# Splitting a second block product once more, and moving masking and att + beta I to another engine, in a four-layer graph network kernel

## The chip, the cores and the metric

The kernel runs on one core of a Trainium2 chip. A core has five engines with a queue each: PE (TensorE, matrix products), DVE (VectorE), ACT (ScalarE), POOL (GpSimd) and SP (SyncE, which here issues all DMAs). Each engine works its own queue strictly in order and waits on semaphores for the others. The metric is the device time of one execution in microseconds; shown is the median of several runs.

## The reference, cut to what matters

```python
def reference(x, adj, W0, bias0, b1, Wq, Wk, Wv, W3, a, beta):   # x: (128, 128, 512), adj: (128, 128), float32
    # layer 0: deg = adj.sum(1); nadj = adj * deg^-1/2 (rows and columns)
    x = layernorm(x + nadj @ (x @ W0) + bias0)
    # layer 1: A = adj @ x, C = adj @ x + b1; out[o, i] = max over j of relu(A[o, j] + (C - A)[o, i])
    x = layernorm(x + out)
    # layer 2: rel = adj.T * (q @ k.T), each row divided by its norm
    x = layernorm(x + rel(x) @ (x @ Wv.T))
    # layer 3: h = x @ W3; e = leaky_relu(s1 + s2.T) * adj; att = softmax(e)
    x = layernorm(x + elu(att @ h + beta * h))
    return x
```

x is 128 matrices of 128 x 512 (nodes by features). Since both weights of layer 1 are the same, C - A is the bias alone, out is the same along each row, and the normalization takes it out again; the kernel folds layer 1 into the variance of the normalization before it (1 + EPS in `var`). In layer 2, q k^T = x (Wq^T Wk) x^T, so one product with a matrix G = Wq^T Wk serves for both. In layer 3, att h + beta h = (att + beta I) h.

## The kernel before, in words

**Groups and steps.** The 128 matrices go in 32 groups of four (GB = 4). `Group` holds the steps of one group, each a method with a short name: y (nadj x), w (times W0), z (times G), r (rel = z x^T), v (times Wv^T), f (rel times v), k (times W3) and h ((att + beta I) times k) are TensorE's; the others are the work around them. "3.ej" in a schedule is step ej of the group that is 3 after the base.

**The order is written out.** HEAD, TURN and TAIL are strings of such steps. The loop at the end (`for base, steps in ...`) runs HEAD, then TURN for each group from FIRST to NG + LAST - 1, then TAIL; each instruction is put on its engine's queue in that order, and nothing reorders it. FIRST is 10 and LAST -5, so TURN runs 17 times, and HEAD and TAIL hold similar stretches written out.

**Block products.** w, z, v and k are products of a 512 x 512 activation (four matrices side by side, two by two blocks of 256 x 256) with a 512 x 512 weight. `Product` computes each by Winograd's form with seven block products in place of eight. The sums of blocks that it takes are on the left side `Left.sum` (GpSimd, tiles S, four of 128 x 512), on the weight side `w_sum` (once, VectorE). `Product.make(i)` does block product i: four matrix products of 128 x 256, each in two instructions. Products 6, 3 and 4 are accumulated onto the banks of 1, 5 and 7 (ONTO). The results are put together from PSUM by c (ScalarE copy), d (VectorE addition), t (ScalarE copy of bank 1 with 6 in it) and u (GpSimd addition).

**The second level.** Block product 2 is split once more by the same form in all of w, z, v and k: `make_small` does four 128 x 128 products (step z2), then ScalarE copies half of the bank to q (`before`, bz2), VectorE makes three operations in the bank (`between`, ez2: two of 128 x 128, one of 128 x 384), and three more 128 x 128 products are accumulated onto it (step z28). The left side's four small sums are `Left.small` (GpSimd, lx2, ly2, ln2; tile L, two buffers); the weight's are `w_small_sums` (VectorE, once).

**Attention of layer 3.** sc multiplies x by two vectors, sums (VectorE, the product itself goes to the scratch tile prod) and leaves s. pw writes s to DRAM and pe reads it back, spread over all partitions (both on SP). pl is the leaky relu (ScalarE), ej the masking with adj (VectorE, L428 by the helper tt), ei the row maximum, ex the exponential, rd the reciprocal of the sum, so0 to so3 att * rden + beta I, one matrix each (VectorE, L1067). at, aw, cat bring the result transposed back through DRAM. In layer 2, sq squares rel for its norm into a scratch tile sq.

**Memory.** PSUM has six rotating banks for products. The sbuf pool `mid` holds e, prod, q, t, rel and the like, one buffer each; aT (the transposed activation) and S have three. Between layers the activation is transposed by VectorE in 32 x 32 squares and put in place by 16 DMAs (xd and nd; `Squares.move`).

**Helpers.** Operations of helpers carry the helper's line: L425 copy (ScalarE), L428 tt (VectorE), L431 pool_tt (GpSimd), L434 inv_sqrt (GpSimd, step pow and others).

Of the kernel before, what the change touches and what calls it, by code (L numbers as in the profile page):

```python
# [46 lines left out]
GB = 4  # L47
# [3 lines left out]
FIRST = 10  # L51
LAST = -5
# [3 lines left out]
0.cy11 1.y10 0.cy01 0.sy0 1.y00 1.cy10 0.ly2 1.y11 1.cy00 1.y01 1.cy11 s.s00 0.w1 1.cy01 0.sy2  # L56
0.w5 s.s01 s.s02 s.s03 0.w7 0.dw1 0.sy3 0.dw5 s.sa0 0.dw7 s.m02 s.sk0 0.w2 s.sa1 0.w6 0.bw2
0.ew2 s.sa2 0.w3 0.tw s.sk2 s.sk1 0.w28 0.dw3 s.sa3 0.w4 0.dw2 0.bi01 s.g1 0.dw4 0.bi00 s.sk3
s.g2 s.cg1 s.vt0 0.bi10 s.vt1 s.g5 0.bi11 3.ld s.dg2 2.ld s.vt2 0.uw01 s.vt3 s.g7 s.cg5 s.vd
s.q00 0.stw0 0.uw10 s.g6 s.dg7 0.uw11 0.stw1 s.g3 s.q01 s.tg 0.stw2 1.sy0 s.g4 0.stw3 1.sy1  # L60
s.dg3 1.w1 0.vaw 1.ly2 s.dg4 1.w5 1.dw1 0.pow s.q02 1.w7 0.nbw 1.dw5 1.sy2 0.apw0 0.apw1 1.w2
1.dw7 s.ug11 0.apw2 1.w6 0.xt0 0.apw3 1.sy3 0.xt1 1.bw2 1.tw 0.xt2 1.bi10 1.w3 0.xt3 1.bi00
1.ew2 0.xd s.sg0 1.w28 s.sv0 1.w4 s.sg1 s.sg2 2.y10 s.sg3 2.y00 2.cy10 s.sv1 s.mg2 2.y11 2.cy00
2.cy11 s.sv2 s.sv3 1.dw3 1.bi11 1.dw2 2.y01 1.bi01 1.dw4 2.cy01 3.y10 s.mv2 3.y00 3.cy10 s.q03
3.y11 3.cy00 s.q10 3.y01 3.cy11 s.q11 0.z1 3.cy01 s.q12 s.q13 s.s30 s.wd 0.cz1 s.bi 0.sx0 s.s31
0.z5 s.s32 s.s33 0.cz5 0.sx1 s.wb s.m32 0.z7 0.lx2 0.dz7 0.sx2 0.z2 s.wc0 1.uw01 0.z6 0.bz2
s.wc1 0.ez2 0.sx3 4.ld 1.stw0 1.uw10 0.z3 1.stw1 1.uw11 0.z28 0.z4 2.sy0 0.dz2 0.tz 1.stw2
0.uz11 0.dz3 0.dz4 0.r0 2.sy1 1.stw3 0.r1 2.ly2 1.vaw 0.r2 0.r3 1.pow 0.v1 0.rm 2.sy2 0.rt 0.sq0
0.sq1 0.wr 0.v5 0.cv1 1.nbw 2.sy3 1.apw0 1.apw1 1.xt0 2.bi10 0.v7 0.cv5 1.xt1 1.apw2 0.cr 2.bi00
0.v2 0.dv7 1.apw3 1.xt2 2.bi11 0.v6 0.bv2 0.sq2 0.ev2 0.sq3 2.bi01 0.v3 1.xt3 0.tv 3.sy0 0.v28  # L70
0.dv3 0.uv11 0.v4 0.dv2 3.sy1 0.f0 1.xd 0.dv4 3.ly2 0.f1 0.f2 3.sy2 0.f3 2.w1 0.rp 3.sy3 0.fa0
2.w5 2.dw1 3.bi10 0.fa1 0.fa2 2.w7 3.bi00 2.dw5 0.fa3 3.bi11 2.w2 2.dw7 2.w6 3.bi01 2.bw2 0.stv0
2.ew2 2.w3 2.tw 0.stv1 2.uw01 0.stv2 2.w28 1.sx0 0.stv3 2.w4 2.dw3 1.sx1 2.dw2 1.z1 2.dw4 1.lx2
2.stw0 1.z5 2.stw1 1.cz1 1.sx2 0.vav 1.z7 2.uw10 1.cz5 1.sx3 1.z2 1.dz7 2.uw11 1.z6 1.bz2 1.ez2
0.pov 1.z3 2.stw2 1.tz 1.uz11 2.stw3 1.z28 2.vaw 1.dz3 2.pow 1.z4 1.dz2 2.nbw 0.nbv 2.apw0 1.r0
1.dz4 2.apw1 2.xt0 1.r1 2.apw2 2.xt1 1.r2 2.apw3 2.xt2 0.apv0 1.r3 2.xt3 0.apv1 1.v1 0.sc00 2.xd
0.apv2 1.rm 0.apv3 0.sc01 1.v5 1.cv1 1.rt 1.sq0 0.sc10 1.sq1 1.v7 0.sc11 1.cv5 1.sq2 0.sc20
1.sq3 1.v2 0.sc21 1.rp 1.dv7 1.v6 1.bv2 1.ev2 1.v3 0.sc30 1.tv 1.uv11 0.sc31 1.v28 1.dv3 1.wr
1.v4 1.dv2 0.pw 3.w1 1.dv4 0.nt0 2.sx0 1.cr 3.w5 0.nt1 2.sx1 3.dw1 0.nt2 3.w7 2.sx2 0.pe 3.dw5
# [205 lines left out]
def kernel(  # L285
# [910 lines left out]
```

## Time and profile before

| | us |
|---|---|
| median of three runs | 2032.43 (2029.44 to 2034.14) |
| the profiled execution | 2034.25 |
| its span | 2032.4 |
| TensorE waiting for others, first 100 us | 13.7 |
| TensorE waiting, 1950 to 2000 | 4.5 |
| queue of SP, time its DMAs take as share of 16 DMA engines | 41.7% |

Where the page names a line, it is one of the listing; "out<-in" are the program's tile names with numbers left out (S_x are the block sums of x, L_x the small sums, p_z a PSUM bank of product z, pl_k one of h, C_z the finished z). The number after x counts instructions. A matmul row's "us" goes from its first instruction's start to the modelled end of its last, and overlaps the next row by some 0.15 us, so that the distance of two starts is its price when TensorE is full. "[2.08 <-PE p_z L567]" is idle time before a row, and what ended it.

### The profile page before, as it was taken

What the parts mean: (1) busy time and instruction counts of PE and PEld (TensorE: products, weight loads), DVE (VectorE), ACT (ScalarE), POOL (GpSimd) and SP (SyncE); (2) the same over time, 40 slices, a digit from 0 to 9 for tenths busy, and PEclk for the clock granted to TensorE, in tenths of its full rate; (3) what the DMA queues carried; (4) which work ended last, traced back from release to release, by engine and by line L of the source; (5) the groups of instructions that cost most, each with busy time, mean ns of one, the idle gap of its engine ahead of it and who ended that gap; (6) DMA issues with size and microseconds to landing.
All of it is one profiled execution on the core that took longest, in us unless ns stands there. A gap on an engine that the chain in (4) does not pass through costs nothing.

```text
span 2032.4 us, 31901 instructions
## 1 busy us (share of the span) xinstructions
PE 2004.9 (99%) x10573; PEld 1713.8 (84%) x10573; DVE 1642.7 (81%) x3464; ACT 807.9 (40%) x1739; POOL 1175.9 (58%) x1223
## 2 busy tenths in 40 slices
PE   9899999999999999999999999999999999999997
PEld 8788888888888888888888888888888888888885
DVE  6777888888887888788888878788778888888787
ACT  2223444443343443343433443433434434343344
POOL 7665664656555666556565556565555664676341
PEclk9999999999999999999999999999999999999999
DMA  7234433543345433434433435333444334344423
GB/s 224 63 56 81 94 89 78 110 91 80 69 99 119 105 89 69 88 92 107 95 87 64 100 93 109 91 74 76 97 101 104 87 63 97 87 102 76 77 64 88
DMA packets 737970, 184.71 MB, mean 91 GB/s; under 512 B 689936, under 2 KB 690320, under 8 KB 737808
## 3 DMA queue, kind: packets, MB, share of 16 engines
q1 hardware_dynamic: 737664, 182.56, 41.7%
q8 instruction: 85, 1.39, 0.3%
q14 instruction: 77, 0.63, 0.1%
q10 hardware_dynamic: 144, 0.13, 0.0%
HBM read 64.55 MB, written 49.87 MB: 56 GB/s over the span
## 4 chain that ended last, share of the span: by engine, by line
PE 93%; DVE 2%; DMA 2%; SPq 1%; ACT 1%; issue 0%; POOL 0%; DVEq 0%; ACTq 0%; POOLq 0%
PE p_z L603 16%; PE p_v L603 15%; PE p_w L603 15%; PE p_k L603 15%; PE pr L942 5%; PE pl_v L991 5%; PE py L773 5%; PE pl_k L991 5%; PE p_z L567 2%; PE p_k L567 2%; PE p_v L567 2%; PE p_w L567 2%; SPq L512 1%; DMA s<-d_s 1%; PE pk L864 1%; DMA d_wa<-wa 0%
## 5 line engine op out<-in xcount | busy, mean ns | idle before, releaser
L833 ACT ACTIVATE x<-x,nb,r 128x512 f32<-128x512 f32 x383 | 284.4, 805 | 77.1 <-DVE nb L827 76.9
L431 POOL TENSOR_TENSOR x<-x,bias_bc 128x512 f32<-128x512 f32 x128 | 161.7, 1275 | 99.7 <-PE py L773 85.2
L431 POOL TENSOR_TENSOR C_k<-C_k,t_k 128x512 f32<-128x512 f32 x31 | 40.0, 1290 | 247.1 <-ACT t_k L425 210.0
L434 POOL TENSOR_TENSOR r<-v,minus_half 128x4 f32<-128x4 f32 (+1 forms) x99 | 99.6, 1006 | 133.9 <-DVE v L819 83.8
L1010 DVE SCALAR_TENSOR_TENSOR prod<-x,wa_bc 128x512 f32<-128x512 f32 x256 | 172.6, 674 | 4.5 <-ACT x L833 0.7
L428 DVE TENSOR_TENSOR x<-p_w,x 128x512 f32<-128x512 f32 x192 | 129.2, 684 | 41.0 <-PE p_w L603 37.0
L431 POOL TENSOR_TENSOR x<-x,t_w 128x512 f32<-128x512 f32 x96 | 120.8, 1284 | 34.7 <-ACT t_w L425 31.1
L425 ACT COPY C_z<-p_z 128x512 f32<-128x512 f32 x64 | 37.4, 584 | 249.2 <-PE p_z L603 249.1
L958 ACT ACTIVATE sq<-rel 128x128 f32<-128x128 f32 x128 | 39.7, 310 | 214.2 <-DVE rel L428 212.3
L773 PEld LDWEIGHTS py<-nadjT,x 128*128 128x128 f32 x1024 | 120.6, 194 | 3.4 <-DVE nadjT L671 0.8
L603 PE MATMUL p_z<-S_x,gq_t 128*128 128x256 f32 x512 | 121.2, 379 | 1.2 <-POOL S_x L431 1.2
L603 PE MATMUL p_w<-w_t,S_y 128*128 128x256 f32 x512 | 122.2, 382 | 0.0
L773 PE MATMUL py<-nadjT,x 128*128 128x128 f32 x1024 | 121.2, 277 | 0.5 <-DVE nadjT L671 0.4
L603 PE MATMUL p_z<-S_x,gq 128*128 128x256 f32 x512 | 121.1, 379 | 0.6 <-POOL S_x L431 0.6
L603 PE MATMUL p_k<-w,S_n 128*128 128x256 f32 x496 | 118.9, 383 | 2.7 <-DVE x L1104 2.7
L603 PE MATMUL p_v<-wvT_t,S_x 128*128 128x256 f32 x512 | 121.0, 379 | 0.0
L603 PE MATMUL p_v<-wvT,S_x 128*128 128x256 f32 x512 | 121.0, 379 | 0.0
L603 PE MATMUL p_w<-w,S_y 128*128 128x256 f32 x512 | 121.0, 379 | 0.0
L603 PE MATMUL p_k<-w_t,S_n 128*128 128x256 f32 x496 | 117.2, 379 | 0.0
L991 PE MATMUL pl_k<-C_k,attT 128*128 128x512 f32 x248 | 111.6, 592 | 0.0
L991 PE MATMUL pl_v<-C_v,relT 128*128 128x512 f32 x248 | 111.5, 592 | 0.0
L603 PEld LDWEIGHTS p_z<-S_x,gq 128*128 128x128 f32 x512 | 97.2, 190 | 14.2 <-POOL S_x L431 1.0
(1857 smaller groups left out, 5281.9 us busy)
## 6 DMA issues: line engine op xcount, KB each, us to landing
out_dram<-x SPq DMA_DIRECT2D x127, 256.0 KB, 2.6
x<-in_x_dram SPq DMA_DIRECT2D x31, 1024.0 KB, 5.3
d_r<-ru SPq DMA_DIRECT2D x31, 256.0 KB, 2.0
relT<-d_r SPq DMA_DIRECT2D x124, 64.0 KB, 2.5
s<-d_s SPq DMA_DIRECT2D x31, 256.0 KB, 5.4
d_a<-au SPq DMA_DIRECT2D x31, 256.0 KB, 2.0
attT<-d_a SPq DMA_DIRECT2D x124, 64.0 KB, 2.5
x<-in_x_dram SPq DMA_DIRECT2D x2, 512.0 KB, 4.5
```

Source lines behind the costliest of these rows:

```text
L425: nc.scalar.copy(o, i)
L428: nc.vector.tensor_tensor(o, a, b, f)
L431: nc.gpsimd.tensor_tensor(o, a, b, f)
L434: nc.gpsimd.tensor_tensor(o, v, minus_half[:, : v.shape[-1]], ALU.pow)
L567: nc.tensor.matmul(self.banks[i][:, r, bass.ts(c, P)], lhsT=lhsT, rhs=rhs, start=(not then and n == 0), stop=(n == len(steps) - 1), skip_g ...
L603: nc.tensor.matmul(ps[:, j, :], lhsT=lhsT, rhs=rhs, start=(i not in ONTO and j == 0 and kc == 0), stop=(j == 1 and kc == 1), skip_group_ch ...
L773: nc.tensor.matmul(o, lhsT=self.x_chunk(b, kc), rhs=nadjT, start=True, stop=True)
L833: nc.scalar.activation(xt, xt, AF.Identity, bias=self.nb[k][:, b : b + 1], scale=self.rstd[k][:, b : b + 1],)
L942: nc.tensor.matmul(self.pr[:, b, :], lhsT=self.whole["z"][:, fc, b // 2, bass.ts(b % 2, P)], rhs=self.xT.chunk(b, fc), start=(fc == 0), st ...
L958: nc.scalar.activation(scratch, self.rel[:, b, :], AF.Square, accum_out=self.n2[:, b : b + 1])
L991: nc.tensor.matmul(ps, lhsT=left[:, b, :], rhs=self.whole[k][:, b, :], start=True, stop=True)
L1010: nc.vector.scalar_tensor_tensor(prod, self.x[:, b, :], 1.0, wide(wa_bc[k]), ALU.mult, ALU.mult, accum_out=self.s[:, k, b : b + 1],)
```

## The change

Six things change:

1. Block product 1 of z and of v (layer 2) is split once more, in the way product 2 is: steps lx1 (GpSimd), z1 as four small products, bz1, ez1, z18; v1, bv1, ev1, v18. Small sums of the weights for it (mg1, mv1) are made once. The L tile is now one buffer of eight small blocks for x.
2. For y and n the small sums no longer have a tile: they lie in block (1, 0) of the transposed activation, which nothing reads after the first-level sums (`Left.room`).
3. Masking (ej) is GpSimd's, and att * rden + beta I is two GpSimd operations over all four matrices (so0, so1) in place of four VectorE operations; in the last group it stays with VectorE.
4. Group 0 has no second level in any product.
5. Scratch tiles go: sc's products go to e, Square's output goes into the PSUM bank pr that rel was read from. Some small tiles have two buffers in place of four.
6. The order is written anew: FIRST = 5, LAST = -6 (TURN runs 21 times). In a turn, TensorE's order was z, y, h, r, w, v, k, f (of groups 4, 5, 2, 4, 5, 4, 3, 4) and is z, r, w, v, y, h, k, f (of groups 4, 4, 5, 4, 6, 2, 3, 4). Product 2 stands third among the block products of z and v, not fourth.

```diff
-FIRST = 10
-LAST = -5
+FIRST = 5
+LAST = -6
...
 TURN = """
-4.z1 4.lx2 3.fa3 3.stv1 4.z5 4.cz1 4.sx2 3.stv2 3.stv3 4.sx3 4.z7 4.cz5 3.vav 3.pov 4.z2 4.dz7
-3.nbv 4.z6 4.bz2 3.apv0 4.ez2 3.apv1 4.z3 3.nt0 4.tz 3.sc00 3.apv2 4.uz11 3.nt1 3.apv3 4.z28
...
+4.z1 1.fin2 3.fa3 4.sx1 1.fin3 4.z5 4.bz1 3.stv0 4.sx2 4.ez1 4.z2 2.so0 3.stv1 4.z18 4.bz2 6.ld
+4.ez2 4.z7 4.cz1 4.sx3 4.cz5 3.stv2 2.so1 4.z6 4.dz7 3.stv3 4.z28 4.tz 2.at 4.z3 4.uz11 4.dz2
+2.aw 3.vav 3.pov 4.z4 4.dz3 3.nbv 3.apv0 2.cat 4.r0 4.dz4 3.apv1 3.nt0 4.r1 3.apv2 3.sc00 3.apv3
+4.r2 3.nt1 4.r3 3.nt2 5.w1 3.nt3 4.rm 3.nd 3.sc01 4.sq0 5.w5 4.sq1 5.dw1 4.sq2 4.rt 4.sq3 5.w7
+4.rp 5.dw5 3.sc10 3.sc11 5.w2 5.dw7 5.w6 5.bw2 3.sc20 5.ew2 5.w3 5.tw 3.sc21 5.uw01 3.sc30 5.w28
+5.uw10 5.dw3 5.w4 5.dw2 4.wr 5.uw11 3.sc31 4.v1 5.dw4 3.pw 4.v5 5.stw0 4.bv1 3.sn0 4.ev1 4.cr
+4.v2 5.stw1 3.sn1 4.v18 4.bv2 5.stw2 4.v7 4.cv1 3.sn2 3.pe 4.ev2 4.cv5 3.ln2 4.v6 5.stw3 4.dv7
+3.sn3 5.vaw 4.v28 4.tv 4.v3 3.pl0 4.dv2 5.pow 3.pl1 3.pl2 3.pl3 4.uv11 4.v4 5.nbw 4.dv3 3.ej
+5.apw0 6.y10 4.dv4 5.apw1 5.xt0 6.y00 6.bi10 5.apw2 3.ei 6.y11 5.apw3 5.xt1 6.bi00 6.y01 6.cy00
+5.xt2 6.cy10 6.bi11 2.h0 5.xt3 6.cy11 5.xd 2.h1 6.cy01 2.em0 6.sy0 3.ex0 2.h2 2.em1 2.ee0 6.sy1
...
-    def w_small(w, m):
-        b = lambda k, j: w[:, 2 + k, bass.ts(j, P)]
+    def w_small(w, m, i):
+        b = lambda k, j: w[:, 2 * (i - 1) + k, bass.ts(j, P)]
...
-    w_m = {k: wts.tile([P, 3, P], F32, name=f"m_{k}") for k in "0gv3"}
-    W2 = {k: w_small(weights[k][0], m) for k, m in w_m.items()}
+    SMALL = ("02", "g1", "g2", "v1", "v2", "32")
+    w_m = {k: wts.tile([P, 3, P], F32, name=f"m_{k}") for k in SMALL}
+    W2 = {k: w_small(weights[k[0]][0], m, int(k[1])) for k, m in w_m.items()}
...
         def small(self, i):
-            a = lambda b, k: self.chunk(b, 2 + k)
-            self.l = big.tile([P, 4, P], F32, tag="L", name=f"L_{self.name}", bufs=2)
-            s = [self.l[:, n] for n in range(4)]
+            a = lambda b, k: self.chunk(b, 2 * (i - 1) + k)
+            s = self.room(i)
...
-            self.smalls = dict(
+            self.smalls[i] = dict(
...
+        def room(self, i):
+            return [self.chunk(2 + n // 2, n % 2) for n in range(4)]
...
+    class Shared(Squares):
+        def room(self, i):
+            if i == 1:
+                self.l = big.tile([P, 2, 4, P], F32, tag="L", name=f"L_{self.name}", bufs=1)
+            return [self.l[:, i - 1, n] for n in range(4)]
...
         def make(self, i, then=None):
-            if i == 2 and self.weight in W2:
+            if i in self.left.smalls:
                 self.make_small(i, then is not None)
...
-            self.xT, self.nT = Squares(f"x_{g}"), Squares(f"n_{g}")
+            self.xT, self.nT = Shared(f"x_{g}"), Squares(f"n_{g}")
...
-            scratch = mid.tile([P, P], F32, tag="sq", name=f"sq_{self.g}_{b}")
             nc.scalar.activation(
-                scratch, self.rel[:, b, :], AF.Square, accum_out=self.n2[:, b : b + 1]
+                self.pr[:, b, :], self.rel[:, b, :], AF.Square, accum_out=self.n2[:, b : b + 1]
             )
...
-            prod = mid.tile([P, D], F32, tag="prod", name=f"prod_{self.g}_{b}_{k}")
+                self.e = mid.tile([P, GB, P], F32, tag="e", name=f"e_{self.g}")
             nc.vector.scalar_tensor_tensor(
-                prod,
+                wide(self.e),
...
         def ej(self):
-            tt(self.e, self.e, adj_b, ALU.mult)
+            pool_tt(self.e, self.e, adj_b, ALU.mult)
...
-        def so(self, b):
-            nc.vector.scalar_tensor_tensor(
-                self.e[:, b, :], self.e[:, b, :], self.rden[:, b : b + 1], beta_i, ALU.mult, ALU.add
-            )
+        def so(self, i):
+            if self.end:
+                e, rden = self.e[:, i, :], self.rden[:, i : i + 1]
+                nc.vector.scalar_tensor_tensor(e, e, rden, beta_i, ALU.mult, ALU.add)
+            elif i == 0:
+                pool_tt(self.e, self.e, self.rden.unsqueeze(2).to_broadcast([P, GB, P]), ALU.mult)
+            else:
+                pool_tt(self.e, self.e, beta_i.unsqueeze(1).to_broadcast([P, GB, P]))
```

In HEAD, the w of group 0 is 1 5 7 2 6 3 4 without 28, y of group 3 moves from before z of group 0 to after its f, and d_wa/a_bc (wd, wb) and the copies wc0, wc1 stand in this order:

```diff
-3.y11 3.cy00 s.q10 3.y01 3.cy11 s.q11 0.z1 3.cy01 s.q12 s.q13 s.s30 s.wd 0.cz1 s.bi 0.sx0 s.s31
-0.z5 s.s32 s.s33 0.cz5 0.sx1 s.wb s.m32 0.z7 0.lx2 0.dz7 0.sx2 0.z2 s.wc0 1.uw01 0.z6 0.bz2
-s.wc1 0.ez2 0.sx3 4.ld 1.stw0 1.uw10 0.z3 1.stw1 1.uw11 0.z28 0.z4 2.sy0 0.dz2 0.tz 1.stw2
...
+1.dw2 2.y01 1.bi01 1.dw4 2.cy01 s.sv3 s.q11 s.q12 s.q13 s.s30 s.wd s.bi 1.uw01 0.z1 s.s32 1.stw0
+0.sx0 0.cz1 1.stw1 0.sx1 0.z5 s.wb s.mg1 0.z2 0.cz5 s.s31 0.sx2 0.z7 0.dz2 s.mg2 s.wc0 0.z6
+0.dz7 0.sx3 s.wc1 4.ld s.s33 0.z3 1.uw10 0.z4 1.uw11 2.sy0 0.tz 1.stw2 0.dz3 0.uz11 0.dz4 0.r0
```

## The prediction

> **What bounds the kernel now.** I read first the busy times, then the engines over the middle of the run, then TensorE's timeline through one turn.
>
> ```profile
> PE 2004.9 (99%) x10573; PEld 1713.8 (84%) x10573; DVE 1642.7 (81%) x3464; ACT 807.9 (40%) x1739; POOL 1175.9 (58%) x1223
> ```
> ```profile
> 600.00:1834.00 1234.00, 1233.22 (x6580) 1057.50 (x6579) 1009.23 (x2118) 503.46 (x1083) 744.72 (x775) 1.00 0.43 91
> ```
> ```profile
> 1023.32 1.89 PE L603 MATMUL p_z<-S_x,gq_t 128*128 128x256 f32 x8
> 1025.05 1.89 PE L603 MATMUL p_z<-S_x,gq 128*128 128x256 f32 x8
> 1026.78 0.38 PE L567 MATMUL p_z<-x_16T,gq 128*128 128x128 f32 x2
> ...
> 1027.66 1.89 PE L603 MATMUL p_z<-S_x,gq_t 128*128 128x256 f32 x8
> ...
> 1031.12 0.38 PE L567 MATMUL p_z<-x_16T,gq 128*128 128x128 f32 x2
> ...
> 1031.79 1.89 PE L603 MATMUL p_z<-x_16T,gq_t 128*128 128x256 f32 x8
> ...
> ```
> The second view (window, then busy us of PE, weight loads, DVE, ACT, POOL; the last columns are granted clock, DMA share, GB/s) leaves TensorE 0.8 us of idle in 1234. Starts in the third view are the prices: a whole block product takes 1025.05 - 1023.32 = 1.73 us, a split one 1027.66 - 1026.78 = 0.88 for its first four products and 1031.79 - 1031.12 = 0.67 for its last three. One turn of the loop repeats after 61.70 us (z starts at 1021.76 and, in the chain of waits, at 1083.46). So time goes with TensorE's work, as long as nobody makes it wait.
>
> **The splits.** A split saves 1.727 - 1.55 = 0.177 us (5.18 us for three whole products in the chain gives 1.727). Product 1 of z and v is split in 31 groups: 62 x 0.177 = 11.0 us. Group 0's four products become whole again: w and z are inside the head below, v and k cost 2 x 0.177 = 0.35.
>
> What a split adds elsewhere is read from these rows:
>
> ```profile
> 1027.91 0.37 ACT L425 COPY q_z<-p_z 128x256 f32<-128x256 f32 x1 [2.08 <-PE p_z L567]
> ```
> ```profile
> 1028.31 0.29 DVE L428 TENSOR_TENSOR q_z<-p_z,q_z 128x128 f32<-128x128 f32 x1 [0.51 <-ACT q_z L425]
> 1028.64 0.90 DVE L428 TENSOR_TENSOR p_z<-p_z,q_z 128x128 f32<-128x128 f32 x2
> ```
> From the end of the four products (1027.66) to the end of the last VectorE operation (1028.64 + 0.90 = 1029.54) it is 1.88 us. Now product 5 (1.73) and the first part of product 2 (0.88) stand between z1 and its second part (18): cover 2.61, slack 0.73. Before ez1 VectorE has fa3 (0.66) and stv0 (0.78), which end about when the copy does, so I count no wait; without the slack, every further 0.69 us operation ahead of it costs what exceeds 0.73, twice a turn.
>
> **Engines off the path.** Per turn VectorE gains two "between" sets, 2 x (0.29 + 0.30 + 0.57) = 2.3 us, and loses the masking (0.72) and four att + beta I (4 x 0.41 = 1.6): nothing in sum, at 82% of the window. ScalarE gains two copies of 0.37. GpSimd gains the four sums of lx1 (1021.20 to 1023.00, 1.8 us) and three 128x512 operations for masking, scaling and adding (no such row; a product with a broadcast operand is nearest to the bias addition, 1.275; bounds 1.27 and 1.72, the slowest such row early on): 1.8 + 3.8 = 5.6 on 37.2 per turn, 70% of it. In GpSimd's order lx1 and the first sum S_x follow pow of layer 3, about 4 us ahead of z1, and the scaling stands between S_x sums with 2 us to spare: no wait. Squares now go to the pr bank, held some 2 us longer; its next user is five allocations on.
>
> ```profile
> L827 DVE SCALAR_TENSOR_TENSOR nb<-mv_k,r 128x4 f32<-128x4 f32 x31 | 24.5, 789 | 7.9 <-POOL r L434 7.9
> ...
> L827 DVE SCALAR_TENSOR_TENSOR nb<-mv_v,r 128x4 f32<-128x4 f32 x32 | 5.2, 162 | 0.0
> ```
> The same instruction takes 162 ns where GpSimd rests and 789 where it works. There are six such small ones a turn; 9% more GpSimd time at half a 1.28 us operation each adds 6 x 0.09 x 0.64 = 0.35 us of VectorE, inside its 18% idle. The Trainium skill ("SBUF — State Buffer", section "SBUF: two separate sides") says that VectorE operations with two SBUF inputs and GpSimd exclude each other for a whole instruction, a rule against giving GpSimd more; it would make this 5.6 us a turn at worst, inside the same idle, so that the sum stays; the rows show it only for the small operations.
>
> **The one thin place: the scores' round trip.** s goes to DRAM (pw) and comes back spread over partitions (pe); ScalarE's prelu waits for it.
>
> ```profile
> 1059.19 0.53 SPq L1023 DMA_DIRECT2D d_s<-s  x1
> 1061.42 0.39 SPq L337 DMA_DIRECT2D x<-in_x_dram  x1
> 1061.91 0.46 SPq L1032 DMA_DIRECT2D s<-d_s  x1
> ```
> ```profile
> 1069.23 1.77 ACT L1038 ACTIVATE e<-s,s 128x128 f32<-128x128 f32 x4 [3.27 <-DMA s<-d_s]
> ```
>
> Before, three out stores and an x load stand ahead of pe on SP's queue, and ScalarE idles 3.27 us. In the changed turn SP's order is n move (16 DMAs), d_r, pw, relT (4), pe, x move (16), stores, x load, d_a, attT. With w starting at 0: the fourth transpose of n is done at 0.7 (VectorE holds dz4, two score products and four transposes after z4), the n move takes 10.7 to 12.0 to issue (1035.17 shows 10.71, another turn 12.04), so d_r goes out at 11.4 to 12.7, w ends at 11.9, relT starts 2.2 later (1054.11 - 1051.87) and takes 2.7: pe at 16.3 to 17.6. From there to the prelu it was 7.3 us in the rows above and 3.6 in another turn (507.60 to 511.17): 19.9 to 24.9. Behind the prelus (1.77) ScalarE has four normalizations (2.93) and then the first copy of y (0.58): that bank is free at 25.2 to 30.2, and the third att product wants it at 11.9 + 11.73 (v) + 3.57 (y) + 1.72 (two products) = 28.9. The ends are 3.7 us early and 1.3 us late in each of 21 turns, 0 to 27 us in all (early earns nothing, TensorE being full). I take the early side of the middle, since no x load lies just ahead of pe any more, and count 2 us for a few late turns. If it is late, masking (behind the prelu, on GpSimd), row maximum, the transposes of x and the em of h follow, with 2 us of room.
>
> **The head.** TensorE's rows up to group 0's r hold most of the idle time that there is:
>
> ```profile
> 22.51 1.06 PE L567 MATMUL p_w<-m,L_y 128*128 128x128 f32 x4 [2.48 <-DVE m L379]
> ...
> 65.09 1.97 PE L603 MATMUL p_z<-x_0T,gq 128*128 128x256 f32 x8 [1.30 <-DVE wprod L700]
> ...
> 81.98 0.77 PE L567 MATMUL p_z<-x_0T,gq 128*128 128x128 f32 x2 [4.66 <-DVE p_z L428]
> ...
> 83.40 3.62 PE L603 MATMUL p_z<-x_0T,gq_t 128*128 128x256 f32 x8
> 86.81 4.07 PE L942 MATMUL pr<-x_0T,C_z 128*128 128x128 f32 x32
> ```
> Both long waits are waits of group 0's second level, which goes. w of group 0 starts at 14.47 and is then 7 x 1.727 = 12.1 us without a wait: it ends at 26.6 in place of 30.77. Group 0's normalization, transposes and x move follow it, so x_0T lands some 4.1 us earlier, at 61. TensorE has come to z at 26.6 + 12.1 (weights' product) + 11.9 (w of group 1) + 3.57 (y of group 2; y of group 3 now comes after f) = 54.2, and idles 6.8 us. After the 4.66 us of idle the rows run slow: 81.98 to 90.72 is 8.74 us for 0.67 + 1.73 + 3.57 = 5.97 of work, 2.8 lost. The Trainium skill ("TensorE: Matmul & The Clock Gate", Part 1) has the clock fall to half after an idle window of about 3.4 us and recover after as much work, which would lose 1.7 and put the sum 1.1 lower. I take 2.8 again: r of group 0 starts at 61 + 12.1 + 2.8 = 75.9, not 86.81. y of group 3 (3.57) is still to be done, so 86.81 - 75.9 - 3.57 = 7.3 us are won. Against it: ScalarE copies t_z behind the two wa copies, which wait 14 us for d_wa and a_bc (65.70 to 79.67); if that ends later than z, or vectors for z come late, up to 5 of it go. Bounds -10 (no slow clock, half the idle) and -2; I take -5, leaning to the late end, as several engines meet here.
>
> **Tail.** Before, it has 0.7 + 1.2 + 2.7 + 1.2 of TensorE idle after 1964, all behind the last two groups' vector work, whose order from f of the last group on is kept: 0, between -3 and +4 (group 30's chain gets 45 us of cover where it had 60).
>
> **Sum**, on the profiled execution (2034.25, of it 2032.4 span and 1.85 around it): -11.0 + 0.35 + 2 - 5 + 0 = -13.65, 2020.6. That execution is 1.8 above the median of the three runs (2032.43), so **2019** against the median.
>
> **Rivals.** (1) The scores' round trip becomes the wait: for it, 27 of the prelus waited on this DMA before, 71.3 us in all; against it, pe now goes out right after relT and without the x load. A mean lateness of 1.0 us in 21 turns gives 2019 - 2 + 21 = 2038, slower; from 0.75 us a turn (15.7) it eats the gain. (2) VectorE is late at z18 and v18: for it, 82% busy and 0.73 us of slack; against it, the order of operations puts only fa3/stv0, dw4/stw0 ahead. At 0.5 us for each of 62 it is 2019 + 31 = 2050; from 0.25 the gain is gone. (3) The head gains nothing and the tail loses 3: 2019 + 5 + 3 = 2027, still faster, or 2031 if the turns lose 4 as well: no change. (4) The second level of product 1 isn't taken: excluded, the built order shows seven 128x128 products for z1 and v1 in groups 1 to 31.
>
> **Chances.** Forecast 0.68, its own range 2009 to 2026; (1) 0.10; (2) 0.07; (3) 0.15. Low end: -11 + 0.35 - 10 - 3 = -23.7, 2008.8. High end: forecast with 0.9 us of lateness a turn (19 - 2), 2036. A change under 0.2% (4 us) can't be told from none, so faster means below 2028.4 and slower above 2036.5: faster 0.78 (forecast and two thirds of (3)), same 0.08, slower 0.14 (most of (1) and (2)).
>
> **What would show it.** Right: turns of 61.35 us in the chain, TensorE's window still without idle, z1 in 0.88 and 0.67; GpSimd at 68 to 70%; no "m" or "p_z" wait in the head, one of 5 to 8 us before z of group 0. Wrong: pl_k waiting for ScalarE's y copy with the prelu waiting for s (rival 1), p_z or p_v waiting for VectorE's p_z (rival 2), granted clock below 1.00 in the loop.

## The result, and the profile after

| | median us | runs | profiled execution | its span |
|---|---|---|---|---|
| before | 2032.63 | 4 | 2034.25 | 2032.4 |
| after | 2021.40 | 4 | 2021.49 | 2019.7 |

The ratio is 0.9947 (95% interval 0.9930 to 0.9964): faster by 0.5%, 11 us; 2019 was forecast.

The busy times of the changed kernel, and its engines over the middle of the run (window, then busy us of PE, weight loads, DVE, ACT, POOL; clock, DMA share, GB/s):

```profile
PE 1992.9 (99%) x10921; PEld 1715.3 (85%) x10921; DVE 1645.2 (81%) x3490; ACT 829.7 (41%) x1797; POOL 1330.2 (66%) x1429
```
```profile
300.00:1650.00 1350.00, 1350.00 (x7480) 1165.91 (x7479) 1106.96 (x2355) 570.26 (x1232) 915.16 (x990) 1.00 0.43 91
```

TensorE now has no idle at all in 1350 us of loop, at full clock. VectorE is at 82% there as before, GpSimd at 68%. One turn is 61.38 us long (the first whole products of w start at 1335.90 and 1397.28 in the chain of waits), 0.32 less than the 61.70 before.

The split product in TensorE's timeline, and the VectorE step between its halves:

```profile
1013.50 0.39 PE L529 MATMUL p_z<-x_16T,gq 128*128 128x128 f32 x2
...
1014.40 1.89 PE L565 MATMUL p_z<-S_x,gq_t 128*128 128x256 f32 x8
1016.12 0.39 PE L529 MATMUL p_z<-x_16T,gq 128*128 128x128 f32 x2
...
1017.02 0.39 PE L529 MATMUL p_z<-x_16T,gq 128*128 128x128 f32 x2
...
1017.69 1.89 PE L565 MATMUL p_z<-S_x,gq 128*128 128x256 f32 x8
```
```profile
1015.19 0.26 DVE L378 TENSOR_TENSOR q_z<-p_z,q_z 128x128 f32<-128x128 f32 x1
1015.49 0.90 DVE L378 TENSOR_TENSOR p_z<-p_z,q_z 128x128 f32<-128x128 f32 x2
```

The halves of product 1 cost 0.90 and 0.67 us. The step between them ends at 1015.49 + 0.90 = 1016.39, 0.63 us before the second half starts at 1017.02: that is the slack of this wait.

The scores' round trip shows in ScalarE's preludes to the softmax (busy us, mean ns, then idle us ahead of them by cause):

```profile
L998 ACT ACTIVATE e<-s,s 128x128 f32<-128x128 f32 x124 | 55.6, 519 | 25.7 <-DMA s<-d_s 24.4 <-DVE st_v L770 1.1
```

ScalarE waits 24.4 us for them in the whole run, where it was 71.3, and nothing on TensorE waits behind it. In the list of DMA issues the median from issue to landing of s is 3.7 us, before 5.4.

The head and the tail in TensorE's timeline:

```profile
14.01 1.89 PE L565 MATMUL p_w<-w,y_0T 128*128 128x256 f32 x8
...
26.10 3.62 PE L565 MATMUL p_g<-wk_sb,wq_sb 128*128 128x256 f32 x16
...
62.71 3.64 PE L565 MATMUL p_z<-x_0T,gq 128*128 128x256 f32 x8 [8.09 <-DMA x_0T<-sq_x]
66.19 1.89 PE L565 MATMUL p_z<-S_x,gq_t 128*128 128x256 f32 x8
...
76.55 3.92 PE L905 MATMUL pr<-x_0T,C_z 128*128 128x128 f32 x32
```
```profile
1963.06 3.60 PE L953 MATMUL pl_k<-C_k,attT 128*128 128x512 f32 x8
1970.54 0.29 PE L896 MATMUL ps<-ident,s 128*128 128x128 f32 x1 [3.88 <-DVE e L972]
1971.91 0.47 PE L896 MATMUL ps<-ident,s 128*128 128x128 f32 x1 [1.07 <-DVE e L972]
1973.37 0.47 PE L896 MATMUL ps<-ident,s 128*128 128x128 f32 x1 [0.99 <-DVE e L972]
1974.83 0.47 PE L896 MATMUL ps<-ident,s 128*128 128x128 f32 x1 [0.98 <-DVE e L972]
1975.10 3.69 PE L565 MATMUL p_k<-w,n_30T 128*128 128x256 f32 x8
1978.58 3.08 PE L565 MATMUL p_k<-w_t,S_n 128*128 128x256 f32 x8
```

In the head w of group 0 runs without a wait, and one wait of 8.09 us for x_0T is left. The product behind it takes 66.19 - 62.71 = 3.48 us in place of 1.73: the clock is low for that long. In the tail there is something new. Four small transposes of s of group 31 wait 6.9 us for VectorE's score products, and two products of group 30 behind them run slow (3.48 and 2.92 us in place of 1.73 each, 2.9 us lost). VectorE does these score products late:

```profile
1967.30 0.70 DVE L936 STREAM_TRANSPOSE au<-e 128x512 f32<-128x512 f32 x1
1967.92 0.65 DVE L1068 SCALAR_TENSOR_TENSOR x<-pl_k,x 128x512 f32<-128x512 f32 x1
1968.50 0.67 DVE L972 SCALAR_TENSOR_TENSOR e<-x,wa_bc 128x512 f32<-128x512 f32 x1
```

They write into e now, and e of group 30 is read until au is made; au itself stands behind group 29's first additions onto x, which wait for pl_k (its start is 1963.06). Before, au and the score products, with a scratch of their own, stood ahead of these additions, and the transposes waited 1.2 us:

```profile
1976.31 0.70 DVE L974 STREAM_TRANSPOSE au<-e 128x512 f32<-128x512 f32 x1
1977.76 0.69 DVE L1010 SCALAR_TENSOR_TENSOR prod<-x,wa_bc 128x512 f32<-128x512 f32 x1 [0.74 <-ACT x L833]
```
```profile
1980.30 3.60 PE L991 MATMUL pl_k<-C_k,attT 128*128 128x512 f32 x8
1983.74 0.70 PE L933 MATMUL ps<-ident,s 128*128 128x128 f32 x3
1985.64 0.32 PE L933 MATMUL ps<-ident,s 128*128 128x128 f32 x1 [1.21 <-DVE prod L1010]
```

To place the difference I cut each profiled span in three: up to the start of w of group 2 (head), from there to the transposes of rel of group 31 (middle), and from there to the end (tail). The same work lies in each part in both kernels.

| us | head | middle | tail | span |
|---|---|---|---|---|
| before | 106.08 | 1857.49 | 68.83 | 2032.4 |
| after | 99.40 | 1846.92 | 73.38 | 2019.7 |
| difference | -6.7 | -10.6 | +4.6 | -12.7 |

### The profile page after: what moved, and what is told of

It is laid out like the page before. It is cut to its first block, busy times and chain, and to the rows that moved or that the text cites. A ratio compares the mean times of both kernels' runs of the same rounds, so it can differ in the third digit from the quotient of the medians.

```text
span 2019.7 us, 32758 instructions
## 1 busy us (share of the span) xinstructions
PE 1992.9 (99%) x10921; PEld 1715.3 (85%) x10921; DVE 1645.2 (81%) x3490; ACT 829.7 (41%) x1797; POOL 1330.2 (66%) x1429
## 4 chain that ended last, share of the span: by engine, by line
PE 97%; SPq 1%; DVE 1%; DMA 0%; issue 0%; ACT 0%; POOL 0%; DVEq 0%; POOLq 0%
PE p_k L565 16%; PE p_w L565 16%; PE p_z L565 14%; PE p_v L565 13%; PE pr L905 6%; PE py L736 6%; PE pl_v L953 5%; PE pl_k L953 5%; PE p_z L529 5%; PE p_v L529 5%; PE p_k L529 2%; PE p_w L529 2%; SPq L465 1%; PE pk L827 1%; DVE e L972 0%
## 5 line engine op out<-in xcount | busy, mean ns | idle before, releaser
L972 DVE SCALAR_TENSOR_TENSOR e<-x,wa_bc 128x512 f32<-128x512 f32 x256 | 173.2, 676 | 3.8 <-ACT x L796 0.9
L384 POOL TENSOR_TENSOR r<-n,minus_half 128x4 f32<-128x4 f32 x32 | 32.4, 1012 | 174.5 <-ACT pr L920 174.5
L963 DVE SCALAR_TENSOR_TENSOR x<-pl_v,r,x 128x512 f32<-128x512 f32 x128 | 90.1, 743 | 39.5 <-PE pl_v L953 38.7
L1061 DVE SCALAR_TENSOR_TENSOR x<-pl_k,x 128x512 f32<-128x512 f32 x127 | 86.8, 688 | 29.7 <-PE pl_k L953 29.4
L565 PEld LDWEIGHTS p_w<-w,S_y 128*128 128x128 f32 x512 | 97.3, 190 | 13.2
```

The lines of the kernel that those rows point to most:

```text
L384: nc.gpsimd.tensor_tensor(o, v, minus_half[:, : v.shape[-1]], ALU.pow)
L565: nc.tensor.matmul(ps[:, j, :], lhsT=lhsT, rhs=rhs, start=(i not in ONTO and j == 0 and kc == 0), stop=(j == 1 and kc == 1), skip_group_ch ...
L963: nc.vector.scalar_tensor_tensor(xt, self.pf[b], self.rnorm[:, b : b + 1], xt, ALU.mult, ALU.add)
L972: nc.vector.scalar_tensor_tensor(wide(self.e), self.x[:, b, :], 1.0, wide(wa_bc[k]), ALU.mult, ALU.mult, accum_out=self.s[:, k, b : b + 1],)
L1061: nc.vector.scalar_tensor_tensor(xt, self.pz[b], 0.0, xt, ALU.max, ALU.add)
```

## The experiments

Each kernel is the changed one with the edit shown. Kernels were measured on several chips, each beside the kernel before, so ratios to it are compared, and the three parts of the spans:

| run | median us | ratio to before (95%) | head | middle | tail |
|---|---|---|---|---|---|
| again (unchanged) | 2024.03 | 0.9948 (0.9936 to 0.9961) | 102.83 | 1846.69 | 72.68 |
| whole1 | 2034.67 | 0.9998 (0.9989 to 1.0006) | 103.45 | 1857.19 | 72.96 |
| mock2 | 2042.82 | 1.0039 (1.0026 to 1.0053) | 102.56 | 1865.80 | 73.34 |
| dve_mask | 2026.49 | 0.9968 (0.9956 to 0.9980) | 99.14 | 1848.77 | 73.59 |
| w0_split | 2029.11 | 0.9971 (0.9961 to 0.9981) | 107.40 | 1846.71 | 73.09 |
| head_y3 | 2026.03 | 0.9958 (0.9945 to 0.9970) | 97.07 | 1854.62 | 72.51 |
| tail_apart | 2026.04 | 0.9955 (0.9942 to 0.9969) | 102.58 | 1847.68 | 76.24 |
| tail_order | 2020.34 | 0.9930 (0.9918 to 0.9942) | 103.12 | 1846.66 | 68.72 |
| tail_order2 | 2021.88 | 0.9938 (0.9925 to 0.9952) | 103.13 | 1846.70 | 69.67 |
| tail_pe | 2020.83 | 0.9939 (0.9925 to 0.9953) | 101.69 | 1846.69 | 70.42 |
| tail_pe_wc | 2020.03 | 0.9935 (0.9922 to 0.9947) | 100.84 | 1846.68 | 70.38 |
| tail_best | 2017.60 | 0.9933 (0.9920 to 0.9947) | 99.93 | 1846.69 | 69.08 |

The middle repeats to 0.3 us wherever its work is the same (but for tail_apart, where TensorE waits once for 0.8 us), the head moves by 4 us between runs of the same code. So an edit is judged by the part that it touches.

**again: the changed kernel itself, as a measure.**

> The changed kernel itself, as the measure for what runs beside it on this chip. Expected: a ratio of 0.9947 to the kernel before, as measured (0.9930 to 0.9964), and in its own trace the stretch from the transposes of rel of group 31 to the end at 73.4 us, w of group 2 to the same transposes at 1846.9 us.

The ratio came out the same. Its head is 3.4 us longer than in the first profile: w of group 0 starts at 14.92 and not 14.01, and waits of 1.4 us (p_w) and 1.5 us (pr, for C_z) stand where there had been 0.5 and none.

**whole1: product 1 of z and v not split.**

```
-  4.z1 ... 4.bz1 ... 4.ez1 4.z2 ... 4.z18 ...   (and lx1; the same for v, in every turn)
+  4.z1 ... 4.z2 ...
```

> The changed kernel with the first block product of z and v made whole again in groups 1 to 31; all else stays. By the rows of the changed kernel a split product takes 0.90 + 0.67 = 1.57 us and a whole one 1.727, so 62 x 0.157 = 9.7 us come back: 2021.4 + 9.7 = 2031.1. By the prediction's term (0.177 each) 11.0 us: 2032.4. Rival: the loop is not bound by TensorE's work alone, since VectorE's two sets a turn and GpSimd's four sums stand in the way of something; then less than 6 us come back (under 2027.4).

Product 1 then multiplies with a block of which a quarter has been overwritten by a difference (the sums for the split are still made in place), so the values are not the reference's; number and shape of the products are those of a whole one. The middle grows by 1857.19 - 1846.69 = 10.5 us, 0.169 us for each of 62 splits, and the ratio by 0.0050 (10.2 us). The rival falls, and the loop's whole gain is TensorE's own work. 0.169 lies between the prediction's 0.177 and the 0.157 of one row.

**mock2: VectorE 1.4 us later at the step between the halves of z.**

```
+        def mock(self):
+            nc.vector.bn_stats(mock, bias_bc)
...
-  ... 4.sx2 4.ez1 4.z2
+  ... 4.sx2 4.mock 4.mock 4.ez1 4.z2
```

> In each of the 21 repeated turns two more VectorE operations (statistics of a constant, 128x512, 0.70 us each, result unused) stand just ahead of the VectorE step between the two halves of z's product 1. By the slack of 0.63 us read from the changed kernel's trace (step ends at 1016.39, second half starts at 1017.02), 1.40 - 0.63 = 0.77 us a turn become a wait of TensorE for p_z: 16 us, 2037 to 2038. If VectorE's lateness adds no wait there, because the step before (statistics behind f) waits anyway, the time stays within 2 us of 2021.4; if there is no slack at all, 29 us come, 2050.

The list of TensorE's waits has (us in total, times, longest):

```profile
PE p_z L530 <- DVE p_z L379: 14.2, 21, 0.7
```

That is 0.68 us in each of 21 turns, all of them at this one place, as the theory has it; both rivals fall. Yet the middle grew by 19.1 us, 0.91 a turn, and not by 16. The timeline shows where the other 0.23 is:

```profile
1088.97 0.38 PE L530 MATMUL p_z<-x_17T,gq 128*128 128x128 f32 x2
...
1092.26 0.39 PE L530 MATMUL p_z<-L_x,gq 128*128 128x128 f32 x2
1093.31 0.46 PE L530 MATMUL p_z<-x_17T,gq 128*128 128x128 f32 x2 [0.67 <-DVE p_z L379]
1093.61 0.39 PE L530 MATMUL p_z<-L_x,gq 128*128 128x128 f32 x2
```

Without a wait such a pair follows after 0.22 us. Here it comes 1.05 after the pair before, 0.83 late, and itself needs 0.30: 0.91 in all, of which the list counts 0.67. It counts from the modelled end of the pair before (1092.26 + 0.39), which overlaps what follows without a wait by 0.17 us; that is the larger part of the difference.

```profile
1092.27 0.90 DVE L379 TENSOR_TENSOR p_z<-p_z,q_z 128x128 f32<-128x128 f32 x2
```

VectorE's step ends at 1093.17, 4.20 us behind the start of z, where it was 2.89 in the changed kernel (1016.39 - 1013.50). So it is 1.31 us later, and TensorE 0.83: by this the slack is 0.48 us, where the prediction worked out 0.73 and the trace of after showed 0.63 by the rows' ends. The 0.14 us from VectorE's end to TensorE's start (1093.31) make up the difference from 0.63.

**dve_mask: masking and att + beta I back on VectorE.**

```
-            pool_tt(self.e, self.e, adj_b, ALU.mult)
+            tt(self.e, self.e, adj_b, ALU.mult)
...
-            elif i == 0:
-                pool_tt(self.e, self.e, self.rden..., ALU.mult)
-            else:
-                pool_tt(self.e, self.e, beta_i...)
+            for b in range(GB) if i else ():
+                nc.vector.scalar_tensor_tensor(e, e, rden, beta_i, ALU.mult, ALU.add)
```

> The changed kernel with masking and att + beta I back on VectorE, as the kernel before had them (0.69 us and four of 0.29 to 0.41 us a turn); GpSimd loses its three operations. The prediction's view: VectorE has 18% idle, and only what stands ahead of the steps between split halves can hurt by more than 0.63 us; the att operations stand between z18 and the addition of product 7 and masking behind the last addition of v, so TensorE waits little: within 3 us of the changed kernel. Rival, that the change could not have been made without GpSimd: VectorE goes from 82% to 86% and is late at the additions that r, f and h need; waits of p_z, pr or pl appear and 10 us or more are added (ratio 0.9997 or more).

The middle grows by 2.1 us over the other runs, 1.7 of it two waits of p_v (at 1800 and 1939); in the window below TensorE has no idle at all. By the ratio it is 4 us (0.9968 against 0.9948, whose intervals overlap). The rival's 10 us aren't there: the change could have been made with masking on VectorE, for 2 to 4 us. Its tail is 73.6 us too, so the tail's loss does not come from making att of group 30 on GpSimd. VectorE's load over the window from 600 to 1650 rises less than the work moved:

```profile
600.00:1650.00 1050.00, 1050.00 (x5816) 907.20 (x5815) 877.64 (x1919) 442.43 (x961) 648.86 (x715) 1.00 0.42 91
```

It is 877.64 us against 861.26 in the changed kernel, 0.96 us for each of 17.1 turns, though the rows of masking and att have 11.5 + 18.8 = 30.3 us there, 1.77 a turn. Most of the difference is one small operation: var of layer 2 has a mean of 149 ns in this window and not 682, 9.1 us in all. The remaining 0.3 us a turn no single row explains.

**w0_split: the second level of w of group 0 put back.**

```
-  ... 0.w2 ... 0.w6 ... 0.dw2 ... 0.w3 0.tw ... s.m02
+  ... 0.ly2 ... s.m02 0.w2 ... 0.w6 0.bw2 ... 0.ew2 ... 0.w3 0.tw ... 0.w28 ... 0.dw2
```

> w of group 0 gets its second level back (product 2 in seven 128x128 products, its weights' sums early as in the kernel before); z, v and k of group 0 stay whole. Theory, as in the prediction: x_0T hangs on the end of w of group 0, so the wait for m (2.48 us before) and the slow clock behind it return and move everything: w of group 0 takes 16.3 us in place of 12.1, z of group 0 starts 4.2 us later and the whole is 4.2 us longer (2025.6 against 2021.4). Rival: x_0T is bound by transfers ahead of it on SP's queue; then the idle before z shrinks from 8.1 to about 4 and the whole grows by less than 1 us.

```profile
PE p_w L529 <- DVE m L327: 2.7, 1, 2.7
```
```profile
68.31 3.75 PE L565 MATMUL p_z<-x_0T,gq 128*128 128x256 f32 x8 [8.10 <-DMA x_0T<-sq_x]
```

w of group 0 runs from 14.25 to 30.81, 16.6 us in place of 12.1. The wait ahead of z is 8.10 us as before, and the head is 4.6 us longer than in the unchanged kernel on the same chip; the ratio gives 4.7. The 8 us of idle do not absorb it: z starts 37.5 us after the end of w of group 0 here, and did so in the unchanged kernel on that chip (27.01 and 64.51).

**head_y3: y of group 3 into that idle time.**

```
-  0.fa2 3.y10 0.fa3 3.y00 3.cy10 ... 3.cy01
+  1.dw4 2.cy01 3.y10 s.sv3 3.y00 3.cy10 3.y11 3.cy00 3.y01 3.cy11 3.cy01
```

> y of group 3 (3.57 us of TensorE) moves from behind f of group 0 to ahead of z of group 0, where TensorE idles 8.09 us for x_0T; nothing else changes. Theory: the head is bound by x_0T alone there, so z still starts at about 62.7, r at 76.5, and w of group 2 starts 3.57 us earlier: 2017.8 (down to 2016 if the shorter idle spares some of the slow clock). Rival: the buffers of x_1T are three, so that with y_3T ahead of it x_1T's move has to wait until v of group 0 has read x_0T (88.8 us plus 14 for the move); then z of group 1 waits for it and less than 1 us is left: 2020.4 or more.

Head and middle together are 1951.69 us; in again, tail_order and tail_apart, whose steps are the changed kernel's up to there, they are 1949.52, 1949.78 and 1950.26. So the 3.57 us did not come; whether the 1.4 to 2.2 us on top are a loss can't be said beside a head that moves by 4. z does start at 61.88 and w of group 2 at 97.07, then VectorE stands:

```profile
107.73 0.71 DVE L459 STREAM_TRANSPOSE sq_n<-x 128x512 f32<-128x512 f32 x1 [3.74 <-DMA x_1T<-sq_x]
```
```profile
111.48 1.20 PE L529 MATMUL p_w<-w,y_2T 128*128 128x128 f32 x4 [4.72 <-DVE p_w L378]
```

That is the rival, by a longer way: with y_3T ahead of it, x_1T moves only when x_0T's buffer is free. Its move is issued at 93.87, as the last product that reads x_0T ends (91.91 + 1.89); in the first profile of the changed kernel it goes out at 88.87, ahead of that product (90.67). Until its move is done, VectorE can't reuse the tile that it is moved from, and the step between w's halves stands behind that in VectorE's order.

**tail_apart: a scratch of their own for the last score products.**

```
-                self.e = mid.tile([P, GB, P], F32, tag="e", ...)
+                tag = "rel" if self.end else "e"
+                self.e = mid.tile([P, GB, P], F32, tag=tag, ...)
...
-  8.at ... 9.sc00 7.ea1 9.sc01 ... 9.sc31
+  9.sc00 9.apv2 7.uk11 9.sc01 ... 9.sc31 7.h2 7.em0 ... 8.at
```

> The last group's score products write into a tile of their own (rel's, which is free by then) and stand earlier in VectorE's order, ahead of the transposes of n and of att of group 30. Theory 1, the shared scratch: in the changed kernel these products had to wait until att of group 30 had been transposed, and TensorE's four transposes of s waited for them, 3.88 + 1.07 + 0.99 + 0.98 = 6.9 us and 3.0 us more of slow clock behind it; freed, they are done some 5 us earlier and 4 to 7 us go: 2014.4 to 2017.4. Theory 2, the tail is longer because group 30's chain has less cover in the new order whatever the scratch: within 1.5 us of 2021.4.

The transposes of s wait only 0.55 us, but the tail is 76.2 us, longer still. Two other waits have come:

```profile
1977.43 3.78 PE L565 MATMUL p_k<-w_t,S_n 128*128 128x256 f32 x8 [3.79 <-DVE x L1070]
...
1993.81 6.61 PE L953 MATMUL pl_k<-C_k,attT 128*128 128x512 f32 x8 [3.35 <-DMA attT<-d_a]
```

The score products pulled forward (8 of 0.69 us) push back what VectorE did there: the additions that free TensorE's banks, and au of group 30 (1976.11 where it was 1967.30), whose transfer then comes late. Neither theory holds as it was put. Sharing alone was not tried without a new order; the next run shows what order does while the scratch stays shared.

**tail_order: the scratch shared as in the change, only the order new.**

```
-  9.sc00 7.ea1 9.sc01 ... 9.sc31 7.ea2 9.pe 8.k1 ... 7.ea3 ... 8.k5 ... 8.k7 ... 8.k2 ... 8.k6
+  9.sc00 7.ea1 9.sc01 7.ea2 8.k1 9.sc10 7.ea3 8.k5 ... 8.k7 ... 8.k2 ... 8.k6 ... 9.sc31 8.tk 9.pe
```

> The scratch stays shared; only the order at the end changes: TensorE's transposes of s of group 31 stand behind the products 1, 5, 7, 2 and 6 of group 30, and the score products stand between the operations that free banks. If the cost is that transposes which wait stand in TensorE's queue ahead of products that are ready, 4 to 7 us go as well: 2014.4 to 2017.4. If the lateness of the scores themselves decides (they lead to the last group's att), the wait only moves to the transposes of att of group 31, and the time stays within 1.5 us of 2021.4.

```profile
1969.95 1.89 PE L565 MATMUL p_k<-w,n_30T 128*128 128x256 f32 x8
...
1977.75 0.49 PE L896 MATMUL ps<-ident,s 128*128 128x128 f32 x3
1980.72 0.32 PE L896 MATMUL ps<-ident,s 128*128 128x128 f32 x1 [2.48 <-DVE e L972]
...
1988.71 3.70 PE L953 MATMUL pl_k<-C_k,attT 128*128 128x512 f32 x8 [3.54 <-DVE C_k L378]
```

The products of group 30 follow at once behind pl_k of group 29, at full clock, and the tail is 68.7 us: 4 to 4.7 less than in the changed kernel, and what the kernel before needed. The two tails as windows, of after and of tail_order (window, busy us of PE, weight loads, DVE, ACT, POOL; clock, DMA share, GB/s):

```profile
1946.32:2019.70 73.38, 57.58 (x227) 41.69 (x225) 54.23 (x125) 31.60 (x69) 19.29 (x21) 0.90 0.29 77
```
```profile
1949.78:2018.50 68.72, 53.87 (x227) 39.35 (x225) 54.77 (x125) 31.85 (x69) 19.23 (x21) 0.97 0.32 82
```

TensorE's idle time falls by 0.95 us only, from 15.80 to 14.85: 6.9 us of waits went, and 2.5 and 3.5 came. Its busy time falls by 3.7: what is won is mostly work that ran slow behind the waits, at a mean clock of 0.90 and now 0.97. That the clock stayed up behind the 3.54 us of idle belongs to it, and the theory did not foresee that. So the order at the end was the tail's loss. The edit moves two things, TensorE's transposes behind products that were ready and VectorE's score products apart, so that additions which free banks come between; which of them counts for how much it does not tell.

**tail_order2, tail_pe, tail_best: is more to be had?** The second moves the transposes of s and VectorE's additions further:

```
-  8.k6 ... 9.pe ... 7.stk0 7.stk1 8.k3 7.stk2 ... 8.k28 ... 8.dk3 ... 8.k4 ... 8.dk2 ... 9.at 8.em3 9.k0
+  8.k6 ... 8.k3 8.uk11 9.sc31 8.k28 8.dk3 8.dk2 9.pe ... 8.k4 7.stk0 8.dk4 7.stk1 ... 9.k0 9.at
```

> The tail with the transposes of s of group 31 behind products 1, 5, 7, 2, 6, 3 and 28 of group 30, the additions of products 3, 2 and 4 ahead of group 29's statistics on VectorE, and the first whole product of group 31 ahead of the transposes of its att. The first reordered tail kept two waits, 2.48 us for the scores and 3.54 us for an addition that stood behind group 29's statistics; if order alone is what costs there, both go and the stretch from the transposes of rel of group 31 to the end falls from 68.7 to 63 to 65 us, that is 8 to 10 us below the changed kernel: 2011 to 2013. If VectorE's total work in the stretch (some 45 us from 1957 on) is the bound, the waits only move, and it stays at 68 to 69 us (2016 to 2017).

The two waits went, and another came (69.7 us):

```profile
1985.92 5.37 PE L953 MATMUL pl_k<-C_k,attT 128*128 128x512 f32 x8 [2.58 <-DMA attT<-d_a]
```

So the third lets TensorE transpose att of group 30 as well (and takes the scratch from tail_apart):

```
         def at(self):
-            if self.end:
+            if self.g >= NG - 2:
                 self.pat = self.transpose("pat", lambda b: self.e[:, b, :])
```

> The second reordered tail, with two more edits: att of group 30 is transposed by TensorE (as the last group's is), not through DRAM, and the last group's score products write into rel's tile, so that they need not wait until TensorE has read e of group 30. Theory: what was left in the second reordered tail is the latency of attT of group 30 (15 us from au to pl_k, 2.6 us of wait and 1.8 us of slow clock), so the stretch from the transposes of rel of group 31 to the end falls from 69.7 to about 65 us, 7 to 8 us below the changed kernel (72.7 on the same chip): ratio 0.991. Rival: VectorE, which is nearly without idle from 1957 to 1985, is the bound; then the stretch stays at 68 to 70 us (ratio 0.993).

pl_k of group 30 starts at 1981.72 without a wait, but the tail is 70.4 us: TensorE then stands ahead of group 31's first product.

```profile
1987.77 3.67 PE L827 MATMUL pk_None<-w,n_31T 128*128 128x512 f32 x8 [2.46 <-issue]
```
```profile
1986.98 0.89 DVE L839 TENSOR_TENSOR w<-w 128x512 f32<-128x512 f32 x2
```

The profile finds no releaser ("issue"), but VectorE ends the subtraction that gives w3 its plain blocks back just then. The last run puts that subtraction earlier and group 29's statistics later:

```
-  8.dk4 7.stk1 9.ei ... 9.so3 8.ee0 8.h3 9.rb ... 9.k1 9.ck0 7.apk0 7.apk1 ... 
+  8.dk4 9.rb 9.ei ... 9.so3 8.ee0 8.h3 ... 9.k1 9.ck0 ... 9.em0 7.stk1 7.stk2 7.stk3 ... 9.jc1 7.apk0 7.apk1 ...
```

> As the kernel with TensorE's transposes for group 30 and the later wa copies, with the order behind group 30's products mended once more: the subtraction that gives w3 its plain blocks back stands ahead of the row maximum of group 31 (it held TensorE's first product of group 31, 2.46 us), and the rest of group 29's statistics and normalizations stand behind the last group's first copies (they held C_k_end, 1.4 and 2.0 us). Theory: the three waits go, 5.9 us and the slow clock with them, and the stretch from the transposes of rel of group 31 to the end falls from 70.4 to 64 to 65 us: ratio about 0.9905. Rival: VectorE is the bound of that stretch, and the waits move once more (68 us or more, ratio 0.9925 or more).

```profile
1983.39 3.60 PE L827 MATMUL pk_None<-w,n_31T 128*128 128x512 f32 x8
...
2001.60 1.25 PE L953 MATMUL pl_k<-C_k_end,attT 128*128 128x512 f32 x2 [3.07 <-ACT C_k_end L375]
```

The first product of group 31 now follows without a wait, and 18 us later one of 3.07 us stands: ScalarE copies C_k_end behind normalizations that wait for statistics. The tail is 69.1 us. In all four orders it lies between 68.7 and 70.4 us while the waits change place, as the rivals of the last three expectations have it. The cause that they give is not shown: VectorE is busy for 53.5 to 54.8 us of these stretches, so that its work as a whole does not fill them. What sets their length stays open. An order that goes below 68.7 was not found, which does not show that there is none.

**tail_pe_wc: ScalarE's wa copies behind its copy of t_z.**

```
-  0.sx2 0.z7 0.dz2 s.mg2 s.wc0 0.z6 ... 0.sx3 s.wc1 ... 0.tz
+  0.sx2 0.z7 0.dz2 s.mg2 0.z6 ... 0.sx3 ... 0.tz s.wc0 s.wc1
```

> As the kernel beside it, and ScalarE's two copies of wa stand behind its copy of t_z of group 0 instead of ahead of it. Theory: these copies wait for a_bc (a round trip through DRAM) and hold t_z, so that r of group 0 waits 1.2 to 1.5 us for C_z; that wait goes, and the time is 1.2 to 1.5 us below the kernel beside it. Rival: the later copies hold squares or C_v of group 0 instead, and the wait moves to f of group 0: no gain.

```profile
78.17 3.73 PE L905 MATMUL pr<-x_0T,C_z 128*128 128x128 f32 x32
```

The wait for C_z is gone, but the kernel beside it had only 0.18 us of it in its profile; the head is 0.9 us shorter (0.3 of it because w of group 0 happens to start earlier) and the median 0.8. In the unchanged kernel's run the wait was 1.5 us, so the edit is worth what the transfer happens to be late.

tail_order (0.9930) and tail_best (0.9933, with the wa copies moved as well) beat both kernels, by 3 to 4 us against the change; their intervals overlap that of the change, and what tells them apart is the tail, 68.7 and 69.1 us where the seven runs with the change's own tail have 72.5 to 73.6.

## Why the prediction came out right, term by term

| term, us | predicted | measured |
|---|---|---|
| 62 splits | -11.0 | -10.5 (whole1); middle in all -10.6 |
| v and k of group 0 whole | +0.35 | within the two parts, not seen apart |
| late scores | +2 | 0 |
| head | -5 (worked out: -7.3) | -6.7 in the pair of profiles |
| tail | 0 (-3 to +4) | +4.6 |
| sum | -13.65 | -12.7 (spans) |

- **Bound.** TensorE's work bounds the loop, as read: no idle, turns of 61.38 us (61.35 forecast).
- **Splits.** The rows priced them to 5%: 0.177 us against 0.169.
- **VectorE's slack.** 0.73 us was worked out from rows of product 2; 0.48 to 0.63 is what there is, and nothing uses it up. VectorE stayed at 82%. Small operations grew by more than thought: the six of a turn (var and shift of three layers) add up to 3.06 us by their means from 600 to 1650, from 2.44, so +0.6 and not +0.35. It cost nothing, being inside the idle.
- **GpSimd.** 708.05 us of the window from 600 to 1650, where it was 620.47: some 5 us more a turn, 5.6 forecast.
- **Rival 1, the round trip.** Not one turn was late, so the 2 us of the forecast were too careful: s lands 3.7 us after its issue by the median, where it was 5.4.
- **Head.** The chain was the right one, and w0_split shows its first link alone (4.6 us). z started at 62.7, not 61, after 8.1 us of idle, not 6.8, and the slow clock took 1.75 us, not 2.8. What came later than reckoned is VectorE's part: ScalarE has normalized x_0 at 44.75, 5.7 us earlier than before (50.45), but the last of its transposes ends at 50.07, only 2.4 us earlier (52.44), since two products for wa (wprod, 0.68 and 1.63 us) stand ahead of them now, and the step between the halves of w of group 1 among them. The rule of the Trainium skill ("TensorE: Matmul & The Clock Gate", Part 1), half the clock after an idle window until about as much work is done, gave 1.7, and here the trace agrees with it better than with the row I took from the kernel before. How much the head saves can't be said closer than some 2 us: nine profiles with the same head have w of group 2 start between 99.1 and 103.5, 102.0 in the mean, so that the gain against the one profile of before is 4.1 by the mean and 6.7 by the pair.
- **Tail, the step that failed.** The prediction says of the tail's work that its "order from f of the last group on is kept: 0". TensorE's order is kept there, VectorE's is not. Before, au of group 30 and the score products of the last group stand ahead of group 29's additions, and au starts 4.0 us ahead of pl_k of group 29 (1976.31 and 1980.30). Now the first of these additions stand ahead of au and of the score products, which have to wait for au as they share e, and au starts 4.2 us behind pl_k (1967.30 and 1963.06). TensorE's transposes of s stand where they were, ahead of group 30's products. The prediction's shorter cover of group 30's chain is part of this; what hangs on that chain through e it did not see. The tail costs 4.6 us by the pair of profiles, just past the upper bound of 4, and 4.2 by the mean of the seven tails.
- **Sum.** That the tail did not upset the forecast is luck: the late scores that were not late (2.0) and the head (1.7 better by the pair, 0.9 worse by the mean) stand on the other side. In the profiled executions the sum is off by 0.9 us (2020.6 and 2021.49); the rest of the way from 2019 to 2021.4 is the 1.8 us taken off because before's profiled execution lay above its median, while that of the changed kernel lies 0.1 above its own.

## What to carry to other kernels

When a scratch tile is merged with a tile that carries data, its writes inherit all the waits of that tile; look where in the schedule the next reader on the bounding engine stands, above all at the end of the run, where no other group's work fills the hole. Where the waiting engine's queue has ready work behind the wait, putting that work first can pay (4 us here, by order alone, most of it time that TensorE no longer spent at the low clock), while pulling the late work forward on another engine made something else late. Before a head or a tail is priced from one profile, compare the same stretch over several runs: the loop repeated to 0.3 us, the head to 4.

## What the runs showed of the hardware

- A wait of TensorE costs more than the list of waits counts: 0.68 us listed, 0.91 lost, in each of 21 turns. Some 0.16 us of that is the modelled end from which the list counts; the rest is the first pair of products behind the wait, which takes 0.30 us and not 0.22.
- The length of an idle stretch does not tell by itself whether the clock falls. Windows that begin where TensorE resumes, the last columns again clock, DMA share and GB/s, of tail_order (3.54 us of idle before it), of tail_order2 (2.58) and of tail_best (3.07):

```profile
1988.70:1992.20 3.50, 3.49 (x8) 1.58 (x9) 3.50 (x9) 2.77 (x5) 0.00 (x0) 1.00 0.79 287
```
```profile
1985.90:1989.00 3.10, 3.08 (x5) 1.33 (x6) 1.45 (x4) 1.82 (x8) 0.00 (x0) 0.69 0.00 0
```
```profile
2001.60:2006.00 4.40, 4.40 (x11) 3.19 (x12) 1.67 (x6) 4.40 (x8) 0.55 (x1) 0.61 0.66 247
```

The longest of the three left the clock at 1.00. The Trainium skill ("TensorE: Matmul & The Clock Gate", Part 1) has the clock fall after an idle window of about 3.4 us, and has that window run freely, which would make such differences possible. No run here shows the window itself; that 2.58 us of idle were enough here and 3.54 were not, the measurement decides.

- A small VectorE operation can be several times shorter when GpSimd does less: with three GpSimd operations a turn gone (dve_mask), var of layer 2 took 149 ns and not 682 in the window from 600 to 1650.
- With the same steps up to there, w of group 0 starts between 13.18 and 15.59 us in twelve profiles; the 64 products of y ahead of it take 7.6 to 9.9 us. The granted clock reads 1.00 from 5.6 to 9 us in the earliest and the latest of them (head_y3 and whole1), though the one starts 29 of these products there and the other 15; the cause stays open.
